# A graph layer's sums move from VectorE into PSUM, at addresses held in registers

## The chip, the cores and the metric

The kernel runs on one core of one Trainium2 chip. The metric is the device time of one execution in microseconds; the time before is the median of three runs. A core has five engines that run side by side and meet at semaphores: TensorE (PE) multiplies matrices and writes its results to a small memory called PSUM, VectorE (DVE) and ScalarE (ACT) work element by element, GpSimd (POOL) here starts the transfers that gather scattered rows, and SyncE (SP) starts the plain transfers. Each engine takes its instructions in the order of the program. In the profile's rows, PEld is the loading of TensorE's stationary operand, and a q behind an engine's name (DVEq, POOLq) is its queue's own work: register loads, register arithmetic, waits.

## The reference

One message-passing layer on a graph of 12500 nodes with 64 features and 212500 edges with 32 features, all in 32-bit floating point, followed by a residual and a normalisation. The edges come sorted by their target node, `col`.

```python
msg_in = concatenate([nodes[row], nodes[col], edge_features], axis=-1)   # 160 wide
messages = relu(msg_in @ mW1 + mb1) @ mW2 + mb2                          # hidden width 128
aggregated = segment_sum(messages, col, num_segments=12500)
upd_in = concatenate([nodes, aggregated], axis=-1)
out = layernorm(nodes + relu(upd_in @ uW1 + ub1) @ uW2 + ub2)
```

The second product of the messages is linear, so the kernel sums the hidden rows of a node's edges first and multiplies once per node. For the bias `mb2` it also needs the number of edges of each node, the counts.

## The kernel before

The edges are cut into 554 groups of 384, each of three tiles of 128. Because the edges are sorted, the targets of a group lie within 32 consecutive nodes (`W`), its window; the first node of each window is known only at run time and is read into registers.

What one group goes through:

- **Gather.** The features of the 384 source nodes are brought into a tile of a ring of 20 groups (`RING`, tiles `own_s`), up to 16 groups ahead (`AHEAD`). POOL starts one indirect transfer per tile of 128 rows (line 165). A slot of the ring may be written again once TensorE has transposed the group that was in it.
- **One-hot rows.** VectorE writes, beside the gathered features, 32 columns that mark each edge's target within the window (`onehot`, line 357). In the kernel before this is done two groups ahead.
- **Turn.** TensorE transposes the three tiles (line 369); ScalarE copies the result into a tile that also holds the edges' features, which SP has loaded (line 380).
- **Hidden.** TensorE multiplies by a matrix whose rows are the first layer's weights and, for the one-hot part, the 32 rows of the already projected target nodes, loaded by SP from `by_dst` at the window's address (`window`, line 349). Line 395 is this product; VectorE applies the ReLU (line 406).
- **Sums.** TensorE multiplies the hidden rows by the one-hot rows (line 423), which gives the sums of the window's nodes, and a column of ones by the one-hot rows (line 428), which gives the counts. A product of 32-bit numbers takes two passes, each a weight load and a matmul row in the profile. VectorE adds both into tables of all nodes in SBUF, `agg` and the row `COUNT` of `xc`, at the window's address (lines 437 and 438).

The order is written out by hand. In step `k` TensorE does the turn of group `k`, the hidden product of group `k - 2` and the sums of group `k - 4` one after the other, with one wait ahead of all three; the last ten groups (`SHORT`) are done one product at a time. What follows on the other engines waits for the end of TensorE's step.

Not every tile is gathered. The features of all nodes also lie in SBUF, one node per column (`xc`), and from step 18 on (`BEGIN`) VectorE and ScalarE copy single columns of it, at addresses that they read into registers, straight into the transposed tile (`fetch`, lines 539 and 541; `registers`, line 520). When 128 such copies have been made, one tile, the first of a group in `COPIED`, needs no gather, and ScalarE copies only the rest of the transposed tile (line 380, in two pieces). VectorE copies 12 and 8 columns per step (`VCOLS`), ScalarE 12 and 12 (`ACOLS`), 44 in all (`COLS`); 180 of the 1661 tiles are copied and 1481 gathered.

When the groups of a chunk of 512 nodes are certainly done (`PLAN`), the chunk's update runs in six stages, one per step: line 448 to 450 on TensorE, a ReLU on ScalarE (456), lines 462 and 463 on TensorE, statistics (471, 472), a root (478) and the scaling (486), and a store. At step 8 (`CHECKED`) some one-off work is done on VectorE: it is checked that all edges lie in their windows (`ordered_edges`). If they did not, a slower program would follow; with these inputs it doesn't.

Of the kernel before, what the change touches and what calls it, by code (L numbers as in the profile page):

```python
# [10 lines left out]
F32 = mybir.dt.float32  # L11
# [9 lines left out]
P = 128  # L21
N = 12500
E = 212500
D = 64
# [22 lines left out]
SHORT = 10  # L47
TIMES = 4
BEGIN = 18
CHECKED = 8  # L50
VCOLS = (12, 8)
ACOLS = (12, 12)
# [10 lines left out]
def plan():  # L63


    import math

    def least(g):
        q = min(1.0, g * GE / E)
        return g * GE * N / E - 6.0 * math.sqrt((E - N) * q * (1 - q)) * N / E - 6  # L70

    chunks, b = [], 0
    for e in [c * CH for c in range(1, N // CH + 1)] + [N]:
        n = e - b
        chunks.append((b, *((P, n // P) if n % P == 0 else (n // 2, 2)),
                       next((g for g in range(G) if least(g) >= e), G)))
        b = e
    return chunks


PLAN = plan()
TABLE = [(b, min(4, (NP - b) // P)) for b in range(0, NP, CH)]
# [6 lines left out]
class Own:  # L89
# [4 lines left out]
    def __init__(self, nc, ctx):  # L94
        def on(name, *shape, of=nc.sbuf_tensor):
            return ctx.enter_context(of(name, list(shape), F32)).ap()

        self.s = [on(f"own_s{i}", P, TG, D + W) for i in range(RING)]
        self.st = [on(f"own_st{i}", P, SB * GE) for i in range(BLOCKS)]
        self.wm = [on(f"own_wm{i}", P, H) for i in range(NW)]  # L100
        self.h = [on(f"own_h{i}", P, TG, H) for i in range(NH)]
        self.ident = on("own_ident", P, P)
        self.one = on("own_one", P, 1)
        self.at = (nc.sbuf_base + 31) // 32 * 32
        self.xc = on("own_xc", P, NP)
        self.agg = on("own_agg", P, NP)

        self.ps = [[on(f"own_ps{i}{k}", P, 512, of=nc.psum_tensor) for k in range(3)]
                   for i in range(2)]


@with_exitstack
def ordered(ctx: ExitStack, tc: tile.TileContext, a, own, ok):
# [73 lines left out]
    nc.vector.memset(eps, EPS)  # L187
    zero = const.tile([P, NP // P], F32, name="zero")
    nc.vector.memset(zero, 0.0)
# [11 lines left out]
    nc.sync.dma_start(xc[D : D + 1, :].rearrange("o (p n) -> o p n", p=P), ones[:, : NP // P])  # L201
    nc.sync.dma_start(xc[COUNT : COUNT + 1, :].rearrange("o (p n) -> o p n", p=P), zero)
    w1b = const.tile([D + 1, H], F32, name="w1b")
# [30 lines left out]
    start_i = const.tile([1, G], I32, name="start_i")  # L234
    nc.vector.tensor_copy(start_i, start_f)
    dlc = const.tile([P, G * TG], F32, name="dlc")
    nc.vector.tensor_copy(dlc, dlc_i)
    for f, (g0, g1) in zip(firsts_f, halves):
        part = dlc[:, g0 * TG : g1 * TG].rearrange("p (g j) -> p g j", j=TG)
        nc.vector.tensor_tensor(  # L240
            part, part, f.unsqueeze(2).to_broadcast([P, g1 - g0, TG]), ALU.subtract)


# [15 lines left out]
    nc.scalar.activation(agg.rearrange("p (a b) -> p a b", a=P),  # L259
                         zero.unsqueeze(1).to_broadcast([P, P, NP // P]), AF.Copy)  # L260
    wc = const.tile([H, H], F32, name="wc")

    starts, rows_at, indices, columns_by = {}, {}, {}, {}
    by_dst = dram.tile([NP, H], F32, name="by_dst")
# [12 lines left out]
    def ordered_edges():  # L277

        off = temp.tile([P, G * TG], F32, name="off")
# [4 lines left out]
        opens = [0, *(closes for *_, closes in PLAN)]  # L284
        for (base, *_), g0, g1 in zip([*PLAN, (N,)], opens, [*opens[1:], G]):
            if g0 < g1:
                nc.vector.memset(low[:, g0:g1], float(base))
        wrong = temp.tile([1, 2, G], F32, name="wrong")
# [3 lines left out]
        nc.vector.tensor_tensor(wrong[:, 0], first_f, low, ALU.is_lt)  # L292
        nc.vector.tensor_tensor(wrong[:, 1], first_f, high, ALU.is_gt)
        nc.vector.tensor_reduce(nwrong, wrong, mybir.AxisListType.XY, ALU.add)
        vps = ups.tile([H, CH], F32, name="u_ps")
# [18 lines left out]
    def places(b):  # L314

        g, n = b * SB, min(SB, G - b * SB)
        if n <= 0:
            return
        _, v = nc.values_load_multi_w_load_instructions(
            start_i[0:1, g : g + n], engines=[ET.DVE], min_val=0, max_val=N - 1,  # L320
            skip_runtime_bounds_check_because="they were clamped to the nodes on the chip",
# [68 lines left out]
    def hidden(g, ps):  # L390
# [11 lines left out]
        def relu(step):  # L402
            hidden_by[g] = step
            h = own.h[g % NH]
            if len(set(sizes)) == 1:
                relu_by[g] = [nc.vector.tensor_scalar(h, pre, 0.0, None, ALU.max)]  # L406
# [9 lines left out]
    def sums(g, ps):  # L416
        h, s = own.h[g % NH], own.s[g % RING]
        sizes = tiles_of(g)
        sg = ps[2][:, : TIMES * W].rearrange("p (t w) -> p t w", w=W)
        counted = ps[2][0:1, TIMES * W :][:, :W]  # L420
        did = []
        for j, p in enumerate(sizes):
            did.append(nc.tensor.matmul(  # L423
                sg, h[:p, j, :],
                s[:p, j, D:].unsqueeze(1).to_broadcast([p, TIMES, W]),
                start=j == 0, stop=j == len(sizes) - 1))
        for j, p in enumerate(sizes):
            did.append(nc.tensor.matmul(counted, own.one[:p], s[:p, j, D:],  # L428
                                        start=j == 0, stop=j == len(sizes) - 1))

        def add(step):
            sums_by[g] = step
            at = bass.ds(starts.pop(g), W)
            count = xc[COUNT : COUNT + 1, at]
            if between:
                between.pop()()
            a = after(nc.vector.tensor_tensor(agg[:, at], sg[:, 0, :], agg[:, at], ALU.add), step)  # L437
            return [a, after(nc.vector.tensor_tensor(count, counted, count, ALU.add), step)]  # L438

        return did, [*relu_by[g], *copy_by[g]], add  # L440

# [137 lines left out]
    inputs(1)  # L579
    onehot(0)  # L580
    onehot(1)
    places(0)
# [5 lines left out]
    made = summed = 0  # L588
    between, held = [], {}

    for k in range(G):
# [4 lines left out]
        if k == CHECKED:  # L596
            addresses(0)
            combined()
            ordered_edges()
# [6 lines left out]
        if k < G - SHORT:  # L606
            between.append(lambda: registers(k, 0))
            step((turn, k), *([(hidden, k - 2)] if k > 1 else []),
                 *([(sums, k - 4)] if k > 3 else []))
            made, summed = max(0, k - 1), max(0, k - 3)  # L610
            if between:
                between.pop()()
            fetch(0)
        else:
# [10 lines left out]
        window(k + SB)  # L625
        onehot(k + 2)
        if k < G - SHORT:
            for part in range(1, len(VCOLS + ACOLS)):
                registers(k, part)
                fetch(part)  # L630
            if k >= BEGIN and (k - BEGIN) % SPAN == 0:
# [335 lines left out]
```

## Time and profile before

| | us |
|---|---|
| median of three runs (lowest 1878.53, highest 1881.24) | 1880.31 |
| the profiled execution | 1876.62 |
| its span, first to last instruction | 1874.9 |
| PE busy | 1429.1 (76%) |
| DVE busy | 1491.0 (80%) |
| ACT busy | 1552.1 (83%) |
| POOL busy | 1399.1 (75%) |

The granted clock of TensorE was 0.967 of full speed on the mean. The numbers of the trace below come from the one profiled execution, which stands 3.7 us under the median; 1.7 us of its time lie outside its span.

A row of a group of instructions reads: line, engine, operation, tile written <- tiles read, shapes, count | busy us, mean ns of one | idle us of the engine just before them, and what ended most of it. Consecutive instructions overlap, so the mean of one is longer than the distance between two. A row of a timeline reads: start, length, engine, line, operation, tiles, shapes, count, and in brackets the idle time before it and what ended it.

### The profile page before, as it was taken

What the parts mean: (1) busy time and instruction counts of PE and PEld (TensorE: products, weight loads), DVE (VectorE), ACT (ScalarE), POOL (GpSimd) and SP (SyncE); (2) the same over time, 40 slices, a digit from 0 to 9 for tenths busy, and PEclk for the clock granted to TensorE, in tenths of its full rate; (3) what the DMA queues carried; (4) which work ended last, traced back from release to release, by engine and by line L of the source; (5) the groups of instructions that cost most, each with busy time, mean ns of one, the idle gap of its engine ahead of it and who ended that gap; (6) DMA issues with size and microseconds to landing.
All of it is one profiled execution on the core that took longest, in us unless ns stands there. A gap on an engine that the chain in (4) does not pass through costs nothing. (4 is left out here: it accounts for less than half of the span.)

```text
span 1874.9 us, 61070 instructions
## 1 busy us (share of the span) xinstructions
PE 1429.1 (76%) x12373; PEld 1252.6 (67%) x12373; DVE 1491.0 (80%) x13140; ACT 1552.1 (83%) x13372; POOL 1399.1 (75%) x1488
## 2 busy tenths in 40 slices
PE   3898878778777778687776786776877777867777
PEld 3886667677676677576665676665656666666665
DVE  2458888888888888887887878878888788787873
ACT  3268998988998988988988889889888888898971
POOL 7777777777777777777777777777777777777773
PEclk9999999999999999999999989999999999999998
DMA  4442222222122212211221212212121212121220
GB/s 126 134 117 61 51 53 49 51 53 52 47 54 53 51 48 54 50 49 47 52 54 46 53 47 52 52 46 54 49 49 50 51 49 53 45 55 48 51 50 22
DMA packets 94294, 104.48 MB, mean 56 GB/s; under 512 B 39230, under 2 KB 61366, under 8 KB 93910
## 3 DMA queue, kind: packets, MB, share of 16 engines
q0 software_dynamic: 47392, 48.60, 11.7%
q1 hardware_dynamic: 45888, 51.46, 9.6%
q14 instruction: 280, 2.29, 0.4%
q8 instruction: 104, 1.70, 0.4%
q10 hardware_dynamic: 630, 0.43, 0.1%
HBM read 90.61 MB, written 9.62 MB: 53 GB/s over the span
## 5 line engine op out<-in xcount | busy, mean ns | idle before, releaser
L165 POOL DMA_INDIRECT own_s<-in_x,src_sb x1481 | 1398.4, 944 | 452.5 <-issue 303.3
L541 ACT ACTIVATE own_st<-own_xc 64x4 uint8 x12560 | 1268.1, 192 | 64.3 <-issue 56.0
L539 DVE COPY own_st<-own_xc 64x4 uint8 x10480 | 893.8, 190 | 20.8 <-issue 1.1
L369 PE MATMUL own_ps<-own_ident,own_s 128*96 128x128 f32 x1661 | 292.3, 287 | 396.8 <-issue 116.7
L395 PE MATMUL own_ps<-own_wm,own_st 128*128 128x128 f32 x3322 | 482.7, 284 | 0.0
L423 PE MATMUL own_ps<-own_s,own_h 128*128 128x128 f32 x3322 | 480.0, 282 | 2.6 <-DVE own_h L406 2.0
L369 PEld LDWEIGHTS own_ps<-own_ident,own_s 128*96 128x96 f32 x1661 | 171.1, 134 | 463.4 <-issue 234.9
L380 ACT ACTIVATE own_st<-own_ps 96x384 f32<-96x384 f32 (+2 forms) x734 | 294.0, 401 | 190.2 <-PE own_ps L428 149.3
L423 PEld LDWEIGHTS own_ps<-own_s,own_h 128*128 128x128 f32 x3322 | 433.4, 199 | 5.0 <-DVE own_h L406 3.8
L395 PEld LDWEIGHTS own_ps<-own_wm,own_st 128*128 128x128 f32 x3322 | 434.4, 199 | 1.8 <-issue 0.8
L406 DVE TENSOR_SCALAR own_h<-own_ps 128x384 f32<-128x384 f32 x553 | 302.0, 546 | 141.4 <-PE own_ps L428 97.3
L437 DVE TENSOR_TENSOR own_agg<-own_ps,own_agg 128x32 f32 x554 | 106.0, 191 | 147.2 <-DVE own_h L406 95.1
L428 PE MATMUL own_ps<-own_s,own_one 128*1 128x32 f32 x3322 | 188.8, 194 | 0.0
L428 PEld LDWEIGHTS own_ps<-own_s,own_one 128*1 128x1 f32 x3322 | 113.6, 83 | 69.1 <-issue 4.9
L438 DVE TENSOR_TENSOR own_xc<-own_ps,own_xc 1x32 f32 x554 | 102.0, 184 | 48.4 <-PE u_ps L450 31.7
L357 DVE TENSOR_TENSOR own_s<-iota,dlc 128x96 f32<-128x96 f32 x554 | 137.4, 248 | 0.7
L331 PE MATMUL u_ps<-w1b,own_xc 65*128 65x128 f32 x196 | 52.0, 416 | 30.9 <-DMA own_wm<-in_mW 16.3
L331 PEld LDWEIGHTS u_ps<-w1b,own_xc 65*128 65x128 f32 x196 | 47.2, 324 | 33.2 <-DMA own_wm<-in_mW 16.2
L462 PE MATMUL u_ps<-u,u 128*128 128x64 f32 (+1 forms) x196 | 63.1, 405 | 0.5 <-ACT u L456 0.5
L463 PE MATMUL u_ps<-same,own_xc 65*128 65x64 f32 (+1 forms) x196 | 62.3, 403 | 0.0
L462 PEld LDWEIGHTS u_ps<-u,u 128*128 128x128 f32 (+1 forms) x196 | 54.2, 325 | 2.4 <-ACT u L456 0.8
L463 PEld LDWEIGHTS u_ps<-same,own_xc 65*128 65x128 f32 (+1 forms) x196 | 54.9, 328 | 0.0
(60 smaller groups left out, 268.2 us busy)
## 6 DMA issues: line engine op xcount, KB each, us to landing
own_st<-in_efT SPq DMA_DIRECT2D x138, 192.0 KB
own_s<-in_x,src_sb POOLq DMA_INDIRECT x1481
own_wm<-by_dst SPq DMA_DIRECT2D x554, 16.0 KB
by_dst<-t SPq DMA_DIRECT2D x24, 256.0 KB
out<-o SPq DMA_DIRECT2D x24, 128.0 KB
own_xc<-in_xT SPq DMA_DIRECT2D x12, 179.2 KB
index<-in_src_copied SPq DMA_DIRECT2D x65, 1.4 KB
dlc_i<-in_dst_cols SPq DMA_DIRECT2D x1, 831.0 KB
```

The source lines that it names most:

```text
L165: nc.gpsimd.indirect_dma_start(out=s[:p, j, :D], out_offset=None, in_=x[:, :], in_offset=bass.IndirectOffsetOnAxis(ap=src_sb[:p, g * TG + ...
L357: places_by[g] = nc.vector.tensor_tensor(own.s[g % RING][:, :, D:], iota.unsqueeze(1).to_broadcast([P, TG, W]), dlc[:, g * TG : (g + 1) * ...
L369: nc.tensor.transpose(xt[:, j * P : j * P + p], s[:p, j, :], ident[:p, :p])
L380: after(nc.scalar.activation(t[r, c : c + n][:, m], xt[r, m], AF.Copy), step))
L395: nc.tensor.matmul(pre[:p, j, :], t[:, c + j * P : c + j * P + p], wm[g % NW], start=True, stop=True)
L406: relu_by[g] = [nc.vector.tensor_scalar(h, pre, 0.0, None, ALU.max)]
L423: did.append(nc.tensor.matmul(sg, h[:p, j, :], s[:p, j, D:].unsqueeze(1).to_broadcast([p, TIMES, W]), start=j == 0, stop=j == len(sizes) - 1))
L428: did.append(nc.tensor.matmul(counted, own.one[:p], s[:p, j, D:], start=j == 0, stop=j == len(sizes) - 1))
L462: nc.tensor.matmul(y[:p, k], u[:, k:q:n], u2, start=True, stop=False)
L463: nc.tensor.matmul(y[:p, k], xc[: D + 1, base + k : base + q : n], same, start=False, stop=True)
L539: by[engine] = nc.vector.tensor_copy(o, x_at)
L541: by[engine] = nc.scalar.activation(o, x_at, AF.Copy)
```

## The change

- The sums and counts are no longer added by VectorE for each group. TensorE's matmuls of line 423 and 428 write into two banks of PSUM (`own.acc`), without starting a new sum, at an address that TensorE holds in a register, so that PSUM itself adds up. Nodes are cut into 56 parts of 224 (`NODES`, `PARTS`); parts alternate between the two banks. The sums of a part lie in the first 256 columns of its bank, its counts in the first row of the other 256 (`HALF`). A part is opened by a matmul of zeros over the 512 columns and closed by one over 32 (`CLOSE`); after the step that closes it VectorE adds the part's 256 columns of sums and of counts into `agg` and `xc`, which is done once per part. The address of a window within its bank is worked out on VectorE (`placed`), for the first 32 groups at the start and for the others at step 8, and read into registers of TensorE (`places`) instead of VectorE's.
- The moving operand of the sums is 32 columns wide instead of four times the same 32 (`TIMES`).
- VectorE copies 12 and 12 columns per step instead of 12 and 8: `COLS` is 48, 196 tiles are copied and 1465 gathered.
- The registers for the first 12 columns of VectorE and of ScalarE are loaded ahead of the step, before the ReLU and the copy that wait for TensorE; they were loaded between the ReLU and the additions on VectorE, and behind the copy on ScalarE.
- The one-hot rows are written six groups ahead (`LEAD`).
- The chunks' updates wait for the parts: the first is due after group 33 (before: 25), the last but one after group 548 (before: 546).
- The check at step 8 has one more comparison and 112 small fills where there were 25.

```diff
-TIMES = 4
+LEAD = 6
+NODES = 224
+HALF = NODES + W
+CLOSE = 32
-VCOLS = (12, 8)
+VCOLS = (12, 12)
...
-        self.ps = [[on(f"own_ps{i}{k}", P, 512, of=nc.psum_tensor) for k in range(3)]
+        self.ps = [[on(f"own_ps{i}{k}", P, 512, of=nc.psum_tensor) for k in range(2)]
                    for i in range(2)]
+        self.acc = on("own_acc", P, 2 * 512, of=nc.psum_tensor)
...
+    def placed(g0, g1):
+        def rounded(t):
+            for by in (1.5 * 2 ** 23, -1.5 * 2 ** 23):
+                nc.vector.tensor_scalar(t, t, by, None, ALU.add)
+            return t
+        part, half = (dlc_i.bitcast(F32)[0:1, i * G :][:, : g1 - g0] for i in (0, 1))
+        at = start_f[:, g0:g1]
+        nc.vector.tensor_scalar(part, at, 1.0 / NODES, 0.5 / NODES - 0.5, ALU.mult, ALU.add)
+        rounded(part)
+        nc.vector.tensor_scalar(half, part, 0.5, -0.25, ALU.mult, ALU.add)
+        rounded(half)
+        nc.vector.scalar_tensor_tensor(at, part, float(512 - NODES), at, ALU.mult, ALU.add)
+        nc.vector.scalar_tensor_tensor(place_i[:, g0:g1], half, -1024.0, at, ALU.mult, ALU.add)
...
     def places(b):
-            start_i[0:1, g : g + n], engines=[ET.DVE], min_val=0, max_val=N - 1,
+            place_i[0:1, g : g + n], engines=[ET.PE], min_val=0, max_val=512 + NODES - 1,
...
     def sums(g, ps):
-        for j, p in enumerate(sizes):
-            did.append(nc.tensor.matmul(
-                sg, h[:p, j, :],
-                s[:p, j, D:].unsqueeze(1).to_broadcast([p, TIMES, W]),
-                start=j == 0, stop=j == len(sizes) - 1))
-        for j, p in enumerate(sizes):
-            did.append(nc.tensor.matmul(counted, own.one[:p], s[:p, j, D:],
-                                        start=j == 0, stop=j == len(sizes) - 1))
+        did, needs = [], [*relu_by[g], *copy_by[g]]
+        for c, (_, opens, _) in enumerate(PARTS):
+            if opens == g:
+                did.append(nc.tensor.matmul(
+                    own.acc[:, c % 2 * 512 :][:, :512], zero, zero[:, :1].to_broadcast([P, 512]),
+                    start=True, stop=False))
+                needs += flushed.pop(c - 2, [])
+        at = starts.pop(g)
+        for j in range(n):
+            did.append(nc.tensor.matmul(own.acc[:, bass.ds(at, W)], h[:, j, :], s[:, j, D:],
+                                        start=False, stop=False))
+        for j in range(n):
+            did.append(nc.tensor.matmul(own.acc[0:1, bass.ds(at + HALF, W)], own.one, s[:, j, D:],
+                                        start=False, stop=False))
...
         def add(step):
-            a = after(nc.vector.tensor_tensor(agg[:, at], sg[:, 0, :], agg[:, at], ALU.add), step)
-            return [a, after(nc.vector.tensor_tensor(count, counted, count, ALU.add), step)]
+            for c, (base, _, closes) in enumerate(PARTS):
+                if closes == g + 1:
+                    m = min(HALF, NP - base)
+                    sums_at = own.acc[:, c % 2 * 512 :]
+                    to = agg[:, base : base + m], xc[COUNT : COUNT + 1, base : base + m]
+                    flushed[c] = [
+                        after(nc.vector.tensor_tensor(o, i, o, ALU.add), step)
+                        for o, i in zip(to, (sums_at[:, :m], sums_at[0:1, HALF : HALF + m]))]
+            return []
...
         if k < G - SHORT:
-            between.append(lambda: registers(k, 0))
+            registers(k, 0)
+            registers(k, len(VCOLS))
             step((turn, k), *([(hidden, k - 2)] if k > 1 else []),
                  *([(sums, k - 4)] if k > 3 else []))
...
-            fetch(0)
+            fetch(0, len(VCOLS))
...
-        onehot(k + 2)
+        onehot(k + LEAD)
```

More of the change, by code (lines that the diff above doesn't have):

```diff
@@ L434, in add @@
[L434 to L440, printed above, removed]
+            for c, (base, _, closes) in enumerate(PARTS):
+                if closes == g + 1:
+                    m = min(HALF, NP - base)
[4 more added lines that the diff above has]
+                        for o, i in zip(to, (sums_at[:, :m], sums_at[0:1, HALF : HALF + m]))]
@@ L442, in update @@
+            return []
+        return did, needs, add
     def update(base, p, n):
```

67 lines of the change are left out of this document (42 added, 25 removed).

## The prediction

> **What bounds the kernel now.** I read the page's engine shares first and they mislead: ScalarE is the fullest engine, and GpSimd (POOL) looks a quarter idle.
>
> ```profile
> span 1874.9 us, 61070 instructions
> PE 1429.1 (76%) x12373; PEld 1252.6 (67%) x12373; DVE 1491.0 (80%) x13140; ACT 1552.1 (83%) x13372; POOL 1399.1 (75%) x1488
> L165 POOL DMA_INDIRECT own_s<-in_x,src_sb x1481 | 1398.4, 944 | 452.5 <-issue 303.3
> ```
>
> The row of the gathers says otherwise: 1398.4 us busy and 452.5 us of gaps make 1850.9 us, the whole span but 24 us. The timeline of POOL alone shows what the gaps are (its first two gathers and its last two):
>
> ```profile
> 2.94 1.15 POOL L165 DMA_INDIRECT own_s<-in_x,src_sb  x1 [1.36 <-DMA src_sb<-in_src]
> 4.40 0.94 POOL L165 DMA_INDIRECT own_s<-in_x,src_sb  x1 [0.31 <-issue]
> ...
> 1850.26 0.95 POOL L165 DMA_INDIRECT own_s<-in_x,src_sb  x1 [0.30 <-DMA own_s<-in_x,src_sb]
> 1851.51 0.90 POOL L165 DMA_INDIRECT own_s<-in_x,src_sb  x1 [0.30 <-DMA own_s<-in_x,src_sb]
> ```
>
> Every gather takes 0.94 us and every gap 0.30 us, whoever is named as its releaser, at 4 us with VectorE asleep as at 1850 us. So (1851.51 - 2.94) / 1480 = 1.249 us is a fixed price per gather, paid 1481 times in an unbroken row.
>
> Does the rest of the kernel follow POOL's pace, or does POOL only happen to be busy as long? The table by stretches answers, first for the gathers, then for TensorE's transposes, three per group of 384 edges (stretch, length, busy time and count, then clock and transfers; the second table has a column for the weight loads too):
>
> ```profile
> 2.90:186.90 184.00, 139.33 (x147) 0.97 0.40 111
> 186.90:686.30 499.40, 377.46 (x400) 0.97 0.21 51
> 686.30:1808.60 1122.30, 848.42 (x899) 0.97 0.20 50
> ```
> ```profile
> 2.90:186.90 184.00, 22.25 (x120) 16.95 (x121) 0.97 0.40 111
> 186.90:686.30 499.40, 84.24 (x481) 47.82 (x482) 0.97 0.21 51
> 686.30:1808.60 1122.30, 178.64 (x1021) 101.75 (x1022) 0.97 0.20 50
> ```
>
> At 186.9 us TensorE has turned 40 groups and POOL has gathered 147 tiles. The first 21 groups have 3 gathers, later ones 3 - 44/128 = 2.656, so 147 is 21 + 84/2.656 = about 52 groups: POOL is 12 groups ahead. In the middle stretch TensorE does 160 groups in 499.4 us, 3.12 us each, while POOL's pace is 2.656 x 1.249 = 3.32 us; 160 x 0.20 = 32 us of lead go. In the last stretch TensorE does 340 groups at 3.30 us: POOL's pace. So the other engines' own pace (3.12) rules early, the gathers rule from about 690 us on, and the end is POOL's end plus a tail of 1874.9 - 1852.4 = 22.5 us.
>
> **The change, part by part.** *Gathers.* A step now copies 48 columns instead of 44, so a 128-column tile leaves the queue every 128/48 = 2.67 steps instead of 2.91. With the same first and last steps 196 tiles are copied instead of 180: 1465 gathers, and 16 x 1.249 = 20.0 us less. POOL needs 2.625 x 1.249 = 3.28 us per group. Nothing covers this: it is the stream that ends last.
>
> The 20 us are kept only if the other engines stay under that pace. Their account stands in the middle stretch (128 groups between 200 and 600 us):
>
> ```profile
> 200.00:600.00 400.00, 317.99 (x2820) 277.92 (x2819) 348.55 (x3160) 364.73 (x3248) 302.48 (x321) 0.97 0.21 51
> L541 ACT ACTIVATE own_st<-own_xc 64x4 uint8 x3064 | 308.7, 192 | 9.6 <-issue 7.9 <-DVE own_h L406 0.4
> L539 DVE COPY own_st<-own_xc 64x4 uint8 x2559 | 218.1, 190 | 4.8
> L406 DVE TENSOR_SCALAR own_h<-own_ps 128x384 f32<-128x384 f32 x128 | 69.6, 544 | 9.7 <-PE own_ps L428 9.0
> L369 PE MATMUL own_ps<-own_ident,own_s 128*96 128x128 f32 x384 | 67.3, 285 | 82.0 <-issue 50.4 <-ACT own_st L380 16.6 <-ACT own_st L541 15.0
> ```
>
> Per group that is TensorE 2.48 us, VectorE 2.72, ScalarE 2.85 busy, and TensorE idles 82.0/128 = 0.64 us at the head of each step.
>
> *VectorE.* It loses the two additions and the arithmetic on their address, gains 4 columns, and a larger flush per part:
>
> ```profile
> L437 DVE TENSOR_TENSOR own_agg<-own_ps,own_agg 128x32 f32 x554 | 106.0, 191 | 147.2 <-DVE own_h L406 95.1
> L438 DVE TENSOR_TENSOR own_xc<-own_ps,own_xc 1x32 f32 x554 | 102.0, 184 | 48.4 <-PE u_ps L450 31.7
> L520 DVEq TENSOR_LOAD <-index x1048: 591/843/1131, 112.9 to 1815.9; - x175
> L319 DVEq TENSOR_LOAD <-start_i x139: 339/344/626, 12.3 to 1841.7; - x139
> ```
>
> Gone: (106.0 + 102.0)/554 = 0.38 us busy. Added: 4 x (218.1 + 4.8)/2559 = 0.35 us. The flush is 56 x 2 additions of 256 columns, between L437's 0.19 (32 columns) and L406's 0.54 (384); I take 0.4, nearer the wide one: 45 us in all, 0.08 us a step. Busy becomes 2.77 us. The register loads run on the queue side: 8 registers take 0.59 us (the minimum of the row), 12 take 0.84, and a step now has two of 12; the load of 4 places (0.34 us, every fourth step) moves to TensorE. If nothing hid them they would add 1.7 us and VectorE would be the bound at 4.5; the copies' row shows 4.8 us of gaps in 2559 copies, and the 147.2 us before L437 are 0.27 us a step where a load stands behind a wait. I take 0.2 to 0.3: about 3.05 us.
> [...]
>
> *ScalarE* keeps 24 columns; its first load moves ahead of the wait for TensorE, worth at most the 7.9/128 = 0.06 us of "issue". Tiles copied in two pieces go from 0.34 to 0.375 of the groups, under 0.01 us.
>
> *One-hot rows* six groups ahead cost the same 554 instructions; they take one thing out of what TensorE's step waits for, as the view of waits has it:
>
> ```profile
> PE own_ps L369 <- DVE own_s L357: 32.2, 37, 1.9
> ```
>
> 32 us over the whole run, inside idle that TensorE has anyway; I count nothing. SP's queue issues the same transfers (its index loads grow from 352 to 384 numbers), POOL's only loses gathers.
>
> *TensorE.* Six passes of each kind take:
>
> ```profile
> 901.40 0.83 PE L395 MATMUL own_ps<-own_wm,own_st 128*128 128x128 f32 x6
> 902.07 0.83 PE L423 MATMUL own_ps<-own_s,own_h 128*128 128x128 f32 x6
> 902.83 0.34 PE L428 MATMUL own_ps<-own_s,own_one 128*1 128x32 f32 x6
> ...
> 1835.03 1.13 PE L448 MATMUL u_ps<-own_agg,wc 128*128 128x512 f32 x2
> ```
>
> The sums' moving operand shrinks from 128 to 32 columns: by L428 that saves up to 0.49 us a step, if the loading of 128 weights did not set the pace; I take nothing. [...]
> New: 56 opening matmuls of 512 columns (1.13 us by L448) and 56 closing ones of 32 (0.1 by L428): 69 us, 0.12 us a step. And six register operations a step, one ahead of each matmul with a moving address. No row of before has one on TensorE. On VectorE they stand ahead of L437 and L438:
>
> ```profile
> L437 DVEq FUSED_REGOPS  x554: 76/76/76, 48.5 to 1860.1; - x185
> L438 DVEq FUSED_REGOPS  x554: 93/93/104, 48.6 to 1861.8; - x185
> ```
>
> Behind other work one costs (48.4 - 31.7)/554 = 0.03 us (L438); right behind a load and a wait up to 0.27 (L437). Six cost 0.18 to 1.6 us a step. I take the low end, hidden, because the six are issued while the nine or so passes ahead of them run, as L438's runs under L437. If that cover is gone TensorE goes from 2.60 to at most 4.2 us.
>
> So VectorE at 3.05, TensorE at 2.60 and ScalarE at 2.85 leave the loop, which waits made 3.12, at 3.05 to 3.15 us, under 3.28. *Start.* At step 8 VectorE gets, at once, eight operations on 522 places, 87 more small memsets, one more comparison and a longer reduction:
>
> ```profile
> 39.25 0.56 DVE L406 TENSOR_SCALAR own_h<-own_ps 128x384 f32<-128x384 f32 x1 [25.33 <-PE own_ps L395]
> ...
> 68.43 0.79 DVE L287 MEMSET low<- 1x25 f32 x24
> 69.69 0.77 DVE L292 TENSOR_TENSOR wrong<-first_f,low 1x554 f32<-1x554 f32 x1
> 71.14 1.29 DVE L294 TENSOR_REDUCE nwrong<-wrong 1x1 f32<-1x1108 f32 x1
> ```
>
> (The same eight on the first 32 places come before all that, in the 25 us in which VectorE waits.) 8 x 0.72 + 87 x 0.033 + 0.77 + 0.65 = 10 us, in which TensorE waits. POOL's lead grows by 10/3.3 = 3 to about 15 groups, under the 20 of the ring, so POOL does not stop. The lead to be eaten is 12 x 3.3 + 10 = 50 us; at 3.12 the loop gains 0.16 us a group and has it after 310 of the 513 groups left.
>
> *Tail.* The next to last chunk's update begins two groups later (548 for 546), so its long block falls closer to the end:
>
> ```profile
> 1843.43 0.68 PE L462 MATMUL u_ps<-u,u 128*128 128x64 f32 x2
> ...
> 1847.16 0.93 PEld L395 LDWEIGHTS own_ps<-own_wm,own_st 128*128 128x128 f32 x6
> ...
> 1857.26 0.42 PE L369 MATMUL own_ps<-own_ident,own_s 128*96 128x128 f32 x2
> ...
> 1861.82 0.19 DVE L437 TENSOR_TENSOR own_agg<-own_ps,own_agg 128x32 f32 x1 [1.29 <-PE own_ps L428]
> 1862.04 0.18 DVE L438 TENSOR_TENSOR own_xc<-own_ps,own_xc 1x32 f32 x1
> ```
>
> That is 3.7 us at most and 0 at least, since both orders hold the same work; I take 1. The last flush is two additions of 224 columns instead of 32 (+0.3 in all), a closing matmul (+0.1), register operations behind a wait in five serial steps (0.6). Tail +2.0.
>
> **Sum.** 1874.9 - 20.0 + 2.0 = 1856.9 us of span, with the 1.7 us around it 1858.6, against the profiled run's 1876.6: -0.96%. The median shown, 1880.31, lies 0.2% above that run; scaled by it, 1862.
>
> **Rivals.**
> *The loop becomes the bound.* In the step after a part closes, the first matmul of the sums waits for VectorE's flush, and VectorE may be a step's columns behind: 56 waits of up to about 2 us, 0.2 us a step, on top of 3.12. Groups 40 to 553 start at 186.9 + 10 and end 18.6 us before the end (1874.9 - 1857.3, the start of the last group's transposes, and 1 for the flush). It decides from (1856.9 - 18.6 - 196.9)/513 = 3.20 us on; at 3.24 the span is 1877.7, no change; at 3.30, 1908 (1914 on the median's scale). For it: only 0.08 us of margin over today's 3.12. Against: VectorE's additions, now behind every step, go.
> *Register operations are not hidden (the other side).* TensorE's queue stops at each. It decides from (3.20 - 2.60)/6 = 0.10 us each; at 0.15, between 0.03 and 0.27, a step takes 3.50 and the span is 196.9 + 513 x 3.50 + 18.6 = 2011, about 2017. For it: nothing like it is in the trace. Against: the 93 ns of the row are run under other work on VectorE.
> *Gain given back at the edges.* The lead passes 20 groups at the start and POOL stops, or the update block lands whole in the tail: 4 to 12 us back, 1866 to 1874.
>
> **Chances.** Forecast 0.62 (its own range 1857 to 1866); loop 0.20 (a quarter each faster and unchanged, half slower); register operations 0.13; edges 0.05. Faster by over 0.2% 0.62 + 0.05 + 0.05 = 0.72, within 0.2% 0.05, slower 0.10 + 0.13 = 0.23; 0.2% is about what this measurement tells from nothing. The range 1856 to 1888 leaves out the register rival and the loop's worst part.
>
> **What would show it.** Right: 1465 gathers still 1.25 us apart to the last, ending near 1832; transposes at about 3.28 us late in the run; TensorE idle at step heads. Wrong: POOL gaps over 0.3 us that wait for TensorE, gaps between the sums' passes, transposes far behind the gathers at the end.

## The result, and the profile after

The changed kernel takes 2255.68 us (2249.30 to 2267.17, 4 runs) where the kernel before takes 1880.46 us beside it: 1.201 times as long, interval 1.199 to 1.203. I had forecast 1862 us. The profiled execution has a span of 2247.6 us, 391 us above the span of 1856.9 us that my sum gave.

The page of the changed kernel: the span, the engine shares, the granted TensorE clock in 40 slices, and the rows of the gathers and of the column copies (busy us and mean ns, then the idle us ahead of them).

```profile
span 2247.6 us, 65262 instructions
PE 2008.8 (89%) x12597; PEld 1758.2 (78%) x12597; DVE 1517.5 (68%) x14321; ACT 1529.4 (68%) x13364; POOL 1384.8 (62%) x1472
PEclk9665757676657675666575776575666757676667
L177 POOL DMA_INDIRECT own_s<-in_x,src_sb x1465 | 1384.0, 945 | 764.0 <-issue 374.8
L592 ACT ACTIVATE own_st<-own_xc 64x4 uint8 x12536 | 1244.7, 193 | 0.2
L590 DVE COPY own_st<-own_xc 64x4 uint8 x12552 | 1024.0, 194 | 31.5 <-issue 14.9
```

The clock line of the kernel before, for comparison:

```profile
PEclk9999999999999999999999989999999999999998
```

The 16 gathers are gone, as forecast (1465), and each still takes 0.945 us. But POOL's idle time is 764.0 us where it was 452.5: it no longer runs without a break. TensorE is busy 89% of the span, more than any other engine, and its clock, 0.9 or more in 38 of the 40 slices before, is between 0.5 and 0.8 in every slice but the first; the mean is 0.673, where it was 0.967. The view of waits names the engine that the others wait for (total us, number of waits, longest; POOL's other gaps are its fixed 0.30 us):

```profile
ACT own_st L417 <- PE own_acc L470: 504.5, 328, 10.1
DVE own_h L445 <- PE own_acc L470: 477.4, 306, 8.4
POOL own_s L177 <- PE own_acc L470: 353.4, 168, 7.5
```

All three wait for TensorE's last pass of a step (the counts, L470). The gathers are a full ring ahead (at 1000 us POOL has gathered 260 groups and TensorE has turned 240) and stop until TensorE frees a buffer.

The timeline of TensorE alone shows what became slow. First a step at half clock, then one at full clock, from the same execution (start, length, passes):

```profile
1000.64 0.63 PE L406 MATMUL own_ps<-own_ident,own_s 128*96 128x128 f32 x2
1001.07 1.48 PE L432 MATMUL own_ps<-own_wm,own_st 128*128 128x128 f32 x6
1002.35 1.32 PE L467 MATMUL own_acc<-own_s,own_h 128*128 128x32 f32 x6
1003.60 0.48 PE L470 MATMUL own_acc<-own_s,own_one 128*1 128x32 f32 x6
1004.01 0.88 PE L406 MATMUL own_ps<-own_ident,own_s 128*96 128x128 f32 x3
```
```profile
1042.08 0.53 PE L406 MATMUL own_ps<-own_ident,own_s 128*96 128x128 f32 x3
1042.45 0.83 PE L432 MATMUL own_ps<-own_wm,own_st 128*128 128x128 f32 x6
1043.12 0.75 PE L467 MATMUL own_acc<-own_s,own_h 128*128 128x32 f32 x6
1043.81 0.34 PE L470 MATMUL own_acc<-own_s,own_one 128*1 128x32 f32 x6
1044.87 0.39 PE L406 MATMUL own_ps<-own_ident,own_s 128*96 128x128 f32 x2 [0.73 <-ACT own_st L417]
```

At full clock the passes are those of the kernel before (0.83 us for the hidden layer, 0.34 for the counts), and the narrowed sums take 0.75 us for 0.83. TensorE has time left and waits 0.73 us for ScalarE. At half clock the unchanged hidden layer (L432) takes 1.48 us for 0.83 and the sums 1.32 for 0.75, at 32 columns nearly as much as the hidden layer at 128; the counts take 0.48 for 0.34. TensorE does not wait in these rows. So nothing that the change put into these steps is slow; the clock under them is.

The table by stretches shows how long the clock stays down and what it does to the pace. Four stretches that follow one another, each between two changes of the passes' speed. First all engines (length, busy us and counts of PE, PEld, DVE, ACT and POOL, then the clock), then the transposes alone, three to a group.

```profile
973.60:1035.10 61.50, 58.90 (x303) 51.07 (x302) 40.53 (x384) 38.93 (x345) 35.42 (x39) 0.52 0.17 37
1035.10:1054.70 19.60, 16.26 (x151) 14.29 (x151) 15.88 (x157) 17.63 (x165) 14.14 (x16) 0.94 0.26 54
1054.70:1150.60 95.90, 93.40 (x496) 82.77 (x494) 64.98 (x622) 64.85 (x577) 57.61 (x62) 0.52 0.19 39
1150.60:1173.90 23.30, 18.58 (x172) 16.42 (x172) 18.19 (x183) 21.14 (x193) 16.83 (x18) 0.94 0.22 46
```
```profile
973.60:1035.10 61.50, 11.32 (x39) 6.08 (x39) 0.52 0.17 37
1035.10:1054.70 19.60, 3.62 (x21) 1.98 (x21) 0.94 0.26 54
1054.70:1150.60 95.90, 19.18 (x66) 10.21 (x66) 0.52 0.19 39
1150.60:1173.90 23.30, 4.10 (x24) 2.25 (x24) 0.94 0.22 46
```

At half clock TensorE is busy 58.90 of 61.50 us and 93.40 of 95.90, and does 13 and 22 groups, 4.73 and 4.36 us each. At full clock it does 7 groups in 19.60 us and 8 in 23.30, 2.80 and 2.91 us each, with 3 to 5 us idle. Counted over the trace from 300 us on: 213 groups in 649 us at full clock, 3.05 us each, and 276 groups in 1266 us at half clock, 4.58 us each. My forecast needed a loop under 3.20 us and said 3.05 to 3.15. At full clock that is what it does; for two thirds of the time it does not have that clock.

That accounts for the loss: 489 groups in 1915 us are 3.92 us each where I had 3.28, which makes 489 x 0.64 = 313 us; and in the first 300 us 62 groups are turned where the kernel before turns 77, 15 x 3.3 = 50 us more. Together 363 of the 391 us.

### The profile page after: what moved, and what is told of

Its sections match the earlier page's. It is cut to its first block, busy times and chain, and to the rows that moved or that the text cites. A ratio compares the mean times of both kernels' runs of the same rounds, so it can differ in the third digit from the quotient of the medians.

```text
span 2247.6 us, 65262 instructions
## 1 busy us (share of the span) xinstructions
PE 2008.8 (89%) x12597; PEld 1758.2 (78%) x12597; DVE 1517.5 (68%) x14321; ACT 1529.4 (68%) x13364; POOL 1384.8 (62%) x1472
## 5 line engine op out<-in xcount | busy, mean ns | idle before, releaser
L177 POOL DMA_INDIRECT own_s<-in_x,src_sb x1465 | 1384.0, 945 | 764.0 <-issue 374.8
L590 DVE COPY own_st<-own_xc 64x4 uint8 x12552 | 1024.0, 194 | 31.5 <-issue 14.9
L467 PEld LDWEIGHTS own_acc<-own_s,own_h 128*128 128x128 f32 x3322 | 620.0, 270 | 150.4 <-DVE own_xc L487 95.9
L467 PE MATMUL own_acc<-own_s,own_h 128*128 128x32 f32 x3322 | 598.5, 328 | 90.3 <-DVE own_xc L487 87.7
L432 PE MATMUL own_ps<-own_wm,own_st 128*128 128x128 f32 x3322 | 668.8, 358 | 0.0
L432 PEld LDWEIGHTS own_ps<-own_wm,own_st 128*128 128x128 f32 x3322 | 619.6, 272 | 4.8 <-issue 1.0
L406 PE MATMUL own_ps<-own_ident,own_s 128*96 128x128 f32 x1661 | 396.1, 364 | 98.8 <-issue 66.5
L406 PEld LDWEIGHTS own_ps<-own_ident,own_s 128*96 128x96 f32 x1661 | 218.2, 164 | 181.0 <-issue 104.9
L470 PE MATMUL own_acc<-own_s,own_one 128*1 128x32 f32 x3322 | 228.6, 215 | 0.0
L470 PEld LDWEIGHTS own_acc<-own_s,own_one 128*1 128x1 f32 x3322 | 140.0, 92 | 29.6
L461 PE MATMUL own_acc<-own_zero 128*128 128x512 f32 x112 | 95.0, 947 | 0.0
```

What stands on the lines that cost most here:

```text
L177: nc.gpsimd.indirect_dma_start(out=s[:p, j, :D], out_offset=None, in_=x[:, :], in_offset=bass.IndirectOffsetOnAxis(ap=src_sb[:p, g * TG + ...
L406: nc.tensor.transpose(xt[:, j * P : j * P + p], s[:p, j, :], ident[:p, :p])
L432: nc.tensor.matmul(pre[:p, j, :], t[:, c + j * P : c + j * P + p], wm[g % NW], start=True, stop=True)
L467: did.append(nc.tensor.matmul(own.acc[:, bass.ds(at, W)], h[:, j, :], s[:, j, D:], start=False, stop=False))
L470: did.append(nc.tensor.matmul(own.acc[0:1, bass.ds(at + HALF, W)], own.one, s[:, j, D:], start=False, stop=False))
L590: by[engine] = nc.vector.tensor_copy(o, x_at)
```

## The experiments

Theory A: the clock depends on how many columns TensorE is fed. A step of the kernel before feeds 3 x 128 for transposes, 6 x 128 for the hidden layer, 6 x 128 for sums and 6 x 32 for counts, 2112 columns; the changed one feeds 6 x 96 = 576 fewer, 1536. Theory B: the register operations, or the waits for the flush, tear holes into TensorE's work, and the clock follows those.

One thing is needed to read the numbers. On the chips of the result and of the runs p1 to p4 the kernel before takes 1877 to 1882 us, at a clock of 0.955 to 0.973. On those of the e, n, q and r runs the same kernel takes 2407 to 2458 us, at 0.85 to 0.88; the kernels nearest to it there (e4, r2) are bound by the loop, not by the gathers. Every ratio below is to the kernel before on the same chip; ratios of the two sorts of chip are not set beside each other. The expectations of e1, e3, e4, e6 and of the q runs were written from the times of the faster sort and met the slower one, those of p1 to p4 the other way round, so their microseconds and clocks could not be met as they stand; what they can be held to is the direction. A run given without an interval is a single execution.

**The narrow stream alone (e1, n1, q1).** The kernel before with

```
-TIMES = 4
+TIMES = 1
```

so that the sums' moving operand is 128x32 for 128x128. No register operation, no flush, no other part of the change.

> The kernel before with one edit: the moving operand of the sums is 32 columns wide instead of the same 32 four times (TIMES 1 for 4). Theory A, the narrow operand lets TensorE's granted clock fall: clock 0.65 to 0.75 instead of 0.967, passes of 128 by 128 at about 0.21 us instead of 0.11, time 2150 to 2300 us. Theory B, the clock falls because register operations and waits for the flush tear holes into TensorE's work: nothing of that is in this kernel, so clock 0.967 and 1880 us.

> The kernel before with its sums streamed once instead of four times (moving operand of 128x32 for 128x128), nothing else; the additions on VectorE and all else stay. A (the clock follows the columns that TensorE is fed): the granted clock falls from the kernel before's by 0.2 to 0.35 and the time rises by over 5%. B (register addresses and flushes are the cause): this kernel has none of them on TensorE, so clock and time stay within 1% of the kernel before.

> The kernel before with its sums streamed once (128x32 for 128x128), nothing else; so far seen only where the kernel before itself took 2448 us. A (the clock follows the columns that TensorE is fed): clock 0.60 to 0.72 and 1.10 to 1.25 times the kernel before's time, about what the whole change costs. B (the register addresses and the waits they bring are the cause): clock and time within 1% of the kernel before's.

Measured: 2597.2 us at clock 0.546; 1.062 times (1.059 to 1.064) at 0.541; 1.064 times (1.061 to 1.067) at 0.545. The clock fell from 0.86 or 0.87 each time, and the time rose by 6%, where B expected both unchanged. The page of the last one (shares, clock, the gathers' row):

```profile
PE 2264.7 (88%) x12373; PEld 2047.7 (80%) x12373; DVE 1517.3 (59%) x13140; ACT 1620.9 (63%) x13372; POOL 1402.0 (55%) x1488
PEclk9985555565555555555555555555555555555556
L165 POOL DMA_INDIRECT own_s<-in_x,src_sb x1481 | 1401.2, 946 | 1061.5 <-PE own_ps L428 629.9
```

Less work on TensorE, 88% busy, and half clock almost throughout, without anything that B needs. The size that I expected in q1 (1.10 to 1.25, at a clock of 0.60 to 0.72) is for the other sort of chip; there this kernel was not run.

**Half of it (e4).** The same line with `TIMES = 2`, 1728 columns a step.

> The kernel before with the 32 columns repeated twice (TIMES 2 for 4). Theory A: a value between, clock 0.75 to 0.95 and 1900 to 2150 us, or, if there is a sharp threshold, one of the two ends. Theory B: 1880 us.

One time, 2483.72 us (before 2447.93), at clock 0.768: between 0.545 and 0.86.

**More than before (p3).** `TIMES = 6`, 2496 columns a step.

> The kernel before with its sums streamed six times instead of four (moving operand of 128x192), so that TensorE is fed 2496 columns a step for 2112. A: the granted clock rises from 0.86 towards 0.95; the time falls by up to 3% if TensorE's pace decides, or stays if the passes grow by as much as the clock gives. B (the clock falls with TensorE's load, as a limit on power would have it): the clock falls below 0.86.

1.0017 times (1.0008 to 1.0027), at clock 0.976 where the kernel before has 0.966. A clock that falls with TensorE's load does not fit: with more columns it is a little higher (0.974 to 0.981 in ten executions, 0.955 to 0.973 in thirteen of the kernel before). The time gains nothing, since at 1880 us the gathers are the bound, and the sums' passes grow (from 480 to 647 us in all).

**Fixed addresses (e3, n4, q3) and the changed kernel on the same sort of chip (r1).** The changed kernel with

```
-        at = starts.pop(g)
+        starts.pop(g)
+        at = max(c for c, (_, opens, _) in enumerate(PARTS) if opens <= g) % 2 * 512
...
-            did.append(nc.tensor.matmul(own.acc[:, bass.ds(at, W)], h[:, j, :], s[:, j, D:],
+            did.append(nc.tensor.matmul(own.acc[:, at : at + W], h[:, j, :], s[:, j, D:],
```

and the counts in the same way: no register operation is left on TensorE. Sums of different groups of a part fall on one another.

> The changed kernel with the sums and counts written at the fixed first column of the part's bank instead of at a register's address, so no register operations on TensorE (the sums of a part fall on one another, so this leaves out placing them). Theory A: nothing changes, clock about 0.67 and 2240 to 2270 us. Theory B: the clock comes back above 0.9 and the time falls below 1900 us.

> The changed kernel with sums and counts at fixed addresses, no register operation on TensorE; sums of different groups of a part fall on one another, so the output is not the reference's. A: clock and time within 2% of the changed kernel's. B: clock and time of the kernel before, or better.

> The changed kernel with sums and counts at fixed addresses, no register operation on TensorE; sums of different groups of a part fall on one another, so the output is not the reference's. A: clock 0.64 to 0.70 and the time within 2% of the changed kernel's 2256. B: clock over 0.9 and a time under 1950.

> The changed kernel as it stands. Where the kernel before takes 1880 us it was 1.195 to 1.201 times as long already, and this only repeats it. Where the kernel before takes 2410 to 2450 us: the narrow stream alone cost 1.064, the columns and loads alone 1.010, the kernel with fixed addresses 1.078. A: 1.06 to 1.09, the sum of the first two and the same as with fixed addresses, at a clock of 0.57 to 0.62. B (the register operations cost of their own): over 1.10.

Fixed addresses: 2632.47 us at 0.587; 1.075 times (1.073 to 1.078) at 0.613; 1.078 times (1.073 to 1.083) at 0.594. The changed kernel itself (r1): 1.079 times (1.075 to 1.083) at 0.592. Their clock lines, fixed addresses (q3) first:

```profile
PEclk9956556657556565655565556555555656655556
```
```profile
PEclk9956556557555565555555556555555655555555
```

Without the register operations the clock stays down and the time is within 1% of the changed kernel's: against that half of B. The waits for the flush are still in these kernels and were not taken out by themselves; that they are not needed for the fall, the narrow stream alone shows. And r1 is nearly the sum of its parts on these chips: 0.064 for the narrow stream and 0.008 to 0.012 for the rest (below) make 0.072 to 0.076 of 0.079.

**The other half alone (n2, q2, r2).** The kernel before with the columns, the loads and the one-hot rows of the change, its sums left four times wide and added by VectorE:

```
-VCOLS = (12, 8)
+VCOLS = (12, 12)
+LEAD = 6
...
-            between.append(lambda: registers(k, 0))
+            registers(k, 0)
+            registers(k, len(VCOLS))
...
-            fetch(0)
+            fetch(0, len(VCOLS))
...
-        onehot(k + 2)
+        onehot(k + LEAD)
```

> The other half of the change alone: 24 columns each on VectorE and ScalarE with their loads ahead of the wait, one-hot rows six groups ahead; the sums and counts stay as they were, four times wide and added by VectorE. A: the clock stays at the kernel before's, 16 gathers fewer, and the time falls by up to 1% (my forecast for the change, 1862 against 1880, if VectorE's additions still fit under the gathers' pace of 3.28 us a group; up to 1% slower if they don't). B or a fault in the columns and loads: clock or time go the way of the whole change, by over 5%.

> The columns, the loads ahead and the one-hot rows six groups ahead, without the change of the sums. A, and my forecast of the other terms: clock 0.96 to 0.97, 16 gathers fewer, and the time falls by 0.2 to 1.1% (20 us of gathers against a VectorE that keeps its additions and gains 0.35 us a step). B: it too goes some way towards 2256.

> The columns, the loads ahead and the one-hot rows six groups ahead, without the change of the sums. Where the kernel before takes 1880 us, with the gathers as its bound: A, and my forecast of the other terms: clock 0.96 to 0.97 and the time 0.2 to 1.1% shorter (16 gathers x 1.249 us = 20 us, if VectorE, which keeps its additions and gains 0.35 us a step, stays under 3.28 us a group; if it does not, up to 2% longer). Where it takes 2410 to 2450 us: 1.007 to 1.013 again.

1.008 (1.006 to 1.010), 1.010 (1.007 to 1.013) and 1.012 times (1.009 to 1.015), at clocks of 0.858, 0.877 and 0.875: the kernel before's clock is kept, which confines the loss of clock to the sums. The gathers' row in r2:

```profile
L166 POOL DMA_INDIRECT own_s<-in_x,src_sb x1465 | 1383.6, 944 | 961.1 <-PE own_ps L429 333.9
```

On these chips POOL waits for TensorE even with the clock kept, so 16 gathers fewer buy nothing here, and q2's expected gain of 0.2 to 1.1% did not come. What costs the 1% I did not separate. Whether this half would have brought my 16 us where the gathers are the bound stays open, since this kernel was run only on chips of the slower sort.

**Columns of zeros (e6, n3, q4, p4).** If it is the columns, columns that do nothing must bring the clock back. The changed kernel with one matmul more a step, in q4

```
+        did.append(nc.tensor.matmul(own.acc[:, c : c + IDLE], h[:, 0, :],
+                                    zero[:, :1].to_broadcast([P, IDLE]), start=False, stop=False))
```

with IDLE = 288, two passes of 288, so 2112 columns a step again. In n3 IDLE is 384 (2304 columns); in e6 the weights are one column of ones and the output one row. p4 is the kernel before with `TIMES = 1` and this matmul into unused columns of PSUM.

> The changed kernel with one more matmul per step: a weight of one column, 288 columns of zeros as the moving operand, added to the counts' row. It streams as many columns (two passes of 288) as the narrowing took away (six of 96), and costs about 0.5 us of TensorE at full clock. Theory A, if streamed columns are what counts, whatever their data and however few weight columns: clock above 0.9, the gathers bound again, 1860 to 1885 us. If zeros or a one-column weight do not count: clock 0.65 and 2250 to 2350 us. Theory B: the added work fills no hole that a wait makes, so 2250 us or more.

> The changed kernel with one matmul more a step: 384 columns of zeros through the weights of the sums, added to the open part of PSUM, so that it changes no sum. It does more work on TensorE. A: the clock comes back to within 0.05 of the kernel before's and the time to within 3% of it, although TensorE has 0.3 to 0.7 us more to do in each step. B: the time rises further above the changed kernel's, by some 0.5 us x 554 = 280 us where TensorE is the bound.

> The changed kernel with one matmul more a step: 288 columns of zeros through the weights of the sums into the open part of PSUM, which changes no sum, so that TensorE is fed 2112 columns a step as in the kernel before. A: the clock comes back to 0.90 to 0.95 and the time from 1.195 to 1.00 to 1.05, TensorE being nearly the bound as in the narrow kernel with such columns (1.037). B: clock and time stay at the changed kernel's or get worse.

> The kernel before with its sums streamed once, and one matmul more a step in its place: 288 columns of zeros through the weights of the sums into unused columns of PSUM, so that TensorE is fed 2112 columns a step again. Nothing reads its result. A: the clock comes back from 0.54 to 0.80 to 0.87 and the time from 1.062 to within 1.03 of the kernel before. B (something else in the narrow sums lowers the clock): it stays at 0.54 to 0.65.

The clock rose as A says, from 0.59 to 0.787 in e6, 0.825 in n3 and 0.792 in q4, but not all the way to the 0.86 or 0.87 of the kernel before there; e6's "above 0.9" and q4's 0.90 to 0.95 were missed. Weights of one column do as well as 128 (0.787 and 0.792). The time came back only in part: 1.055 (1.050 to 1.060), 1.067 (1.063 to 1.071) and 1.063 (1.059 to 1.066), from 1.079. So n3's expected clock (within 0.05 of the 0.859 before) was met and its time (within 3%) was missed, as was q4's 1.00 to 1.05: TensorE has the extra passes to do (451.6 us of them in e6, 601.5 in n3). On the chip where the gathers are the bound, p4 took 1.037 times (1.031 to 1.043) at 0.928, the time a little over the 1.03 that I expected. Its page:

```profile
PE 1786.7 (92%) x13481; PEld 1477.7 (76%) x13481; DVE 1480.0 (77%) x13140; ACT 1552.4 (80%) x13372; POOL 1400.2 (72%) x1488
PEclk9679999899999999999899999898898999899997
L424 PE MATMUL own_ps<-own_s,own_h 128*128 128x32 f32 x3322 | 444.1, 272 | 2.0 <-DVE own_h L407 1.4
L431 PE MATMUL own_ps<-zero,own_h 128*128 128x288 f32 x1108 | 440.7, 481 | 0.0
```

The narrow sums and the full clock stand together here. The price is in the same lines: the sums narrowed from 128 to 32 columns still take 444.1 us (480 before), the zeros take 440.7 more, and TensorE is busy 92%. It falls behind the gathers, which still run without a break (457.4 us of gaps, 452.5 before): the last of them ends at 1858.4 us, and TensorE needs 73 us more, where the kernel before needs 22.5.

**The kernel before, profiled (p1), and the changed one, again (p2).**

> The kernel before as it stands, profiled on the chip of this stage. It shows which engine bounds it here: if the gathers still do, POOL has a gather every 1.25 us without a break; if the loop of the other engines does, POOL waits for TensorE and TensorE, VectorE and ScalarE set the pace at about 4.3 us a group. Both theories expect a granted clock of 0.85 to 0.87 as in its other executions here.

> The changed kernel as it stands, on the chip of this stage. A (the clock follows the columns that TensorE is fed): a clock of 0.55 to 0.62 and a time within 2% of the same kernel at fixed addresses (2632), since the register operations cost nothing. B (the register operations cost): over 3% slower than at fixed addresses.

1876.62 us at 0.966 and 1.195 times (1.186 to 1.203) at 0.673: both as in the result, and neither at the clock expected from the slower chips (0.85 to 0.87, and 0.55 to 0.62). In p1 the gathers run without a break (452.5 us of gaps, as in the profile before), so they bind the kernel before here.

All kernels in one table: columns of a step x 554 groups / span of the profiled execution, update and opening passes left out.

| run | columns a step | span, us | columns per us | clock |
|---|---|---|---|---|
| r1, the change | 1536 | 2622.3 | 325 | 0.592 |
| q3, fixed addresses | 1536 | 2601.0 | 327 | 0.594 |
| q1, before, narrow | 1536 | 2560.3 | 332 | 0.545 |
| p2, the change | 1536 | 2252.7 | 378 | 0.673 |
| e4, before, two times | 1728 | 2482.0 | 386 | 0.768 |
| e6, the change with zeros | 2112 | 2602.0 | 450 | 0.787 |
| q4, the change with zeros | 2112 | 2574.3 | 455 | 0.792 |
| r2, the rest alone | 2112 | 2435.2 | 480 | 0.875 |
| n3, the change with more zeros | 2304 | 2603.7 | 490 | 0.825 |
| p4, narrow with zeros | 2112 | 1931.9 | 606 | 0.928 |
| p1, before | 2112 | 1874.9 | 624 | 0.966 |
| p3, before, six times | 2496 | 1878.6 | 736 | 0.976 |

The clock follows the columns that are fed in a microsecond, whichever kernel feeds them and on either sort of chip, with two exceptions (q1, n3). Part of this goes round in a circle, since a slower clock lengthens the span; but the columns of a step are set by the program alone. They are not all that counts: n3 feeds more than r2, in a step and in a microsecond, and has 0.825 for 0.875. Whether zeros in one long pass count for less than columns spread over the step was not separated.

On the chips of the result, then, the changed kernel loses its clock (p2) and narrow sums keep most of it when the columns are given back (p4). That the narrow sums alone bring the loss, and the rest of the change does not, was shown on the slower sort only.

No kernel run here was faster than the kernel before.

## Why the prediction was wrong

*TensorE's clock: the step that failed.* The part on TensorE priced the narrowing at "up to 0.49 us a step" and took nothing for it. The saving was small indeed (0.83 to 0.75 us at full clock). But every duration in the sum, 0.11 us a pass among them, had been read at a granted clock of 0.97, and I carried them to a kernel that feeds 27% fewer columns a step as though the clock were a constant. It was 0.673. For two thirds of the time (1266 of 1915 us) a pass took (1002.35 - 1001.07)/6 = 0.21 us, and a group, updates included, 4.58 us on TensorE alone, where I had 2.60. I had quoted the clock in every stretch and never asked what holds it up. No rival had it either; both that end slower put a wait or a register operation in this place. The loop did become the bound, as the first of them says, but at 3.92 us a group and through the clock, not through the flush.

Nothing in the program said that the wide sums had a use; three of their four copies are never read, and I counted them as saved work only.

The records of the granted clock in the changed kernel's trace are 0.5 or 1, in steps of 3.41 us. A busy TensorE did not bring the clock back: in the stretch from 1054.70 to 1150.60 us it is busy 97% by its rows (93.40 of 95.90 us), and its passes are slow throughout (mean clock 0.52). The clock went with columns streamed more nearly than with time occupied: 32 columns behind a load of 128 weights occupy nearly as long as 128 do (1.32 and 1.48 us above).

*Gathers: right.* 1465, 0.945 us each; the 20 us were there and lay off the path, since POOL waited for TensorE.

*The loop at 3.05 to 3.15: right at full clock* (3.05).

*Register operations: right.* The row of those ahead of the sums, on TensorE's queue, and the runs with fixed addresses:

```profile
L467 PEldq FUSED_REGOPS  x1661: 37/42/42, 42.3 to 2230.6; - x185
```

42 ns each (51 ahead of the counts, L470), done while earlier passes run (1640 of the 1661 ahead of the sums and all ahead of the counts lie within TensorE's busy time); 1.079 with and 1.075 to 1.078 without.

*Flush: sized right, not the cause.* Who waits for the flush, by its line:

```profile
L487 DVE TENSOR_TENSOR own_agg<-own_acc,own_agg x56: 393/414/425, 112.7 to 2232.6; 128x256 f32<-128x256 f32 x55, 128x224 f32<-128x224 f32 x1
  PEld own_acc L467: 95.9, 39
```

0.41 us an addition (I took 0.4), and 95.9/554 = 0.17 us a step of waiting (the rival said 0.2).

*VectorE's loads: about right.* I took 0.2 to 0.3 us a step for register loads that show. The load behind the one-hot rows hardly does: the copies' row above has 31.5 us of gaps in all, 0.06 us a step. The load ahead of the ReLU does: counted over the trace (477 such loads), it ends on the mean 0.23 us after what VectorE does last in the step before, at full clock as at half. Together that is 0.29 us a step. At half clock it costs nothing, since the ReLU waits longer for TensorE.

*Start: too dear.* I said 10 us at step 8, in which TensorE waits. VectorE's block, the first of the new operations, and the last operation of the block in the changed kernel and then in the kernel before:

```profile
59.70 0.41 DVE L258 TENSOR_SCALAR dlc_i<-start_f 1x522 f32<-1x522 f32 x1
...
75.43 0.14 DVE L338 TENSOR_SCALAR ok<-nv 1x1 int32<-1x1 f32 x1
```
```profile
72.72 0.14 DVE L301 TENSOR_SCALAR ok<-nv 1x1 int32<-1x1 f32 x1
```

The block ends 2.7 us later: VectorE comes to it 2.3 us earlier (59.22 for 61.52 us), and 2.01 us of it were a wait before. TensorE then waits 3.25 us for it, where it waited 0.17. The tail cannot be judged, since the last gather ends at 2149.6 us, 98 us before the span does.

## What to carry to other kernels

Durations of TensorE hold at the clock at which they were read (the hidden layer's six passes took 0.83 us at full clock and 1.48 at half), so before a change takes columns away from it, even useless ones, compare what it feeds per microsecond before and after (here 624 and 378) and price the loop at half clock as well. Busy time does not show it: 76% busy went with a clock of 0.97, and 89% with 0.67. Here a narrow moving operand behind a full load of weights saved almost no time (0.75 us a step for 0.83, at full clock), and the clock fell with it (from 0.87 to 0.545 in q1), so copies that nobody reads can be the cheapest way to keep the clock: giving the columns back as zeros instead took 1.037 times as long (p4).

## What the runs showed of the hardware that I had not expected

How the clock falls and comes back, counted over the traces from 300 us on: in the kernel before it drops 28 times, mostly some 10 us after the first pass of a chunk's update, and is back after one or two steps of 3.41 us every time but the last. In the changed kernel it drops 42 times, 12 to 107 us after an update's first pass, and stays down for 10 to 96 us. The clock dropped before the change too; what the changed kernel loses above all is the quick return.

The two sorts of chip: the same kernel takes 1877 us on one and 2447 on another. (Each chip was used in one set of runs only, so that it is the chip is likely, not shown.) ScalarE's column copies, line 541, in p1 and then in q1, where their program is the same:

```profile
L541 ACT ACTIVATE own_st<-own_xc 64x4 uint8 x12560 | 1268.5, 192 | 64.5 <-issue 57.8
```
```profile
L541 ACT ACTIVATE own_st<-own_xc 64x4 uint8 x12560 | 1311.5, 191 | 262.8 <-issue 254.1
```

A copy takes the same 0.19 us; what differs is 200 us more in which ScalarE waits for nothing that the profile shows. In the trace of n2, on such a chip, some of it is stretches of 3 to 4 us in which ScalarE starts only one instruction every 0.72 us: 191 of its instructions and 155 of SP's start 0.69 to 0.75 us after the one before, where p1 has 12 and 4. What causes them I did not find. On those chips the loop takes 4.2 us a group at a clock of 0.88 even with wide sums (r2, from 800 to 1600 us), so half clock has less to add there; the narrow stream's 1.06 there and the change's 1.20 here are not two sizes of one thing.
